# Score matrices of five pairs of key tiles per inner block of layer 2: seven quarter products in place of eight (Strassen), summed on VectorE

## The chip, the cores and the metric

The kernel runs on one core of a Trainium2 chip. The metric is the device time of one execution in microseconds (us), taken as the median of several runs. A profile of one further execution gives the time of every instruction on each engine: TensorE (PE for matmuls, PEld for its weight loads), VectorE (DVE), ScalarE (ACT), GpSimd (POOL), and the DMA queues, most of which are issued by SyncE (SP).

## The reference

Four graph layers are applied to 3327 nodes with 256 features. Each is an attention over the same adjacency matrix, followed by a residual sum and a layer norm. Cut to layer 2, which the change concerns:

```python
def _L2_gnn_ref(x, adj, Wq, bq, Wk, bk, Wv, bv):
    q = x @ Wq.T + bq
    k = x @ Wk.T + bk
    v = x @ Wv.T + bv
    scores = q @ k.T / sqrt(256)
    scores = where(adj > 0, scores, -9e15)
    attention = softmax(scores, axis=-1)
    return elu(attention @ v)

x = layernorm(x + _L0_gnn_ref(...))
x = layernorm(x + _L1_gnn_ref(...))
x = layernorm(x + _L2_gnn_ref(x, adj, ...))
x = layernorm(x + _L3_gnn_ref(...))     # three attention layers of its own
```

All of it is computed in float32. Layers 1 and 3 build their attention weights from sums of two vectors, without a score matrix; layers 0 and 2 need one.

## The kernel before

**Tiles.** The 3328 padded nodes are NT = 26 key tiles of 128 and NB = 7 query blocks of CH = 512 (the last one has 256). A layer is a loop over blocks `b`, and in a block over key tiles `j`; `steps` lists all (layer, block, tile) in order. "Pair p" below means key tiles 2p and 2p+1, of which a block has 13. "Inner blocks" are b = 1 to 5.

**One pair in layer 2.** `weights2` (L556) computes the transposed scores of one key tile with all queries of the block: two float32 matmuls (one for each half `h` of the 256 features, L563) of 128x128 keys from `FT` by 128x512 transformed queries `g`, summed in one PSUM bank `ps`. TensorE executes each float32 matmul as two instructions, so a pair takes 8 of them. ScalarE turns the bank into `ex` with an exponential (L571), and VectorE multiplies by the 0/1 mask into `e` (`masked`, L477). When both tiles of a pair are there, `sums` (L720, its four operations at L727 to L730) makes the four sums S1 to S4 of the quarters of `e`, 128x256 each, on VectorE. `products` (L751, its matmuls at L779) then multiplies the weights by the values `v`, as seven Strassen products, 14 matmuls of 128x128 or 128x129 (28 instructions), into the four banks `po` of the block. The sums of the values, `tsums`, are fetched from HBM by `fetch_tsum`.

**A block.** At a block's end `finish` runs as a generator, one `yield` further with each step of the next block. It joins the products (`joined`, L787, twelve or so VectorE operations that read PSUM and so free the `po` banks), then does ELU, residual and layer norm, and the scores of layer 3 (L591). `block2` (L515) prepares the transformed queries `g` of the next block from step 14 on (matmuls at L522, gT at L529, a maximum at L537, and a chain of small operations that ends in `off`).

**What sets the order.** The main loop calls `make_to(s + LA + 1)` with LA = 2, so that the weights of a tile are issued three steps ahead of the step that uses them. `make` (L1305) issues the weights and, at an odd tile, the sums. Only the first steps stand in an order written by hand; after that a scheduler orders each engine's instructions from the program's order, its own cost model and the free buffers. Each engine works through its instructions in that order. In layer 2 TensorE's order is: 8 score instructions of pair p+1, 28 product instructions of pair p-1 or p, and so on in turn.

**Buffers.** PSUM has two pools: `ps_o`, five banks, four of which a block's `po` occupy, and `ps_b`, three banks through which everything else rotates (`bank`, L66: `ps`, `pgq`, `psr`, `pn`). In SBUF the tag "a" (three buffers) holds the exponentials, "e" (five) the weights, "acc" (two) the sums `ssum`, "stage" (four) and "x4k" (two) larger intermediates. The pool `wts` holds weights of the layers, under tags of which "scratch0", "scratch1", "scratch2", "w_l1_w" and "w_l2_wvt" are 128x512 float32 each and not in use through the inner blocks of layer 2; "scratch1" and "w_l1_w" are loaded again for the last attention of layer 3 (`setup3`).

Of the kernel before, what the change touches and what calls it, by code (L numbers as in the profile page):

```python
# [8 lines left out]
F32 = mybir.dt.float32  # L9
# [4 lines left out]
AF = mybir.ActivationFunctionType  # L14
ALU = mybir.AluOpType
# [4 lines left out]
P = 128  # L20
D = 256
H = 128
LA = 2
CH = 512
# [9 lines left out]
def gnn_stack(ctx: ExitStack, tc: tile.TileContext, a: dict, N: int, out: bass.AP):  # L34
# [8 lines left out]
    nc = tc.nc  # L43
    NT = (N + P - 1) // P
    NP = NT * P
    NB = (NP + CH - 1) // CH
# [3 lines left out]
    def bw(b):  # L50
        return min(CH, NP - b * CH)
# [6 lines left out]
    wts = ctx.enter_context(tc.tile_pool(name="wts", bufs=1))  # L58
    cols = ctx.enter_context(tc.tile_pool(name="cols", bufs=2))
    mpool = ctx.enter_context(tc.tile_pool(name="mpool", bufs=2))  # L60
    work = ctx.enter_context(tc.tile_pool(name="work", bufs=2))
# [4 lines left out]
    def bank(name):  # L66
        return ps_b.tile([P, CH], F32, tag="pb", name=name)
# [3 lines left out]
    start = tc.manual_schedule(  # L71
        engines={engines.PE, engines.Activation, engines.DVE, engines.Pool}
    )
# [30 lines left out]
    FT = [big.tile([P, 2, CH], F32, name=f"ft{g}") for g in range(NB)]  # L104
# [28 lines left out]
    def rsqrt(dst, v, n, eng=nc.vector, tag="rs"):  # L133


        g = cols.tile([P, n], I32, tag=tag + "_g", name="rs_g")
        eng.tensor_scalar(g, v.bitcast(I32), -0.5, MAGIC, ALU.mult, ALU.add)
        y = g.bitcast(F32)
        vh = cols.tile([P, n], F32, tag=tag + "_v", name="rs_v")
        eng.tensor_scalar(vh, v, -0.5 * 0.375**3, None, ALU.mult)  # L140

        def step(out, q, c, f):

            if eng is nc.vector:
                eng.scalar_tensor_tensor(out, q, c, f, ALU.add, ALU.mult)
            else:
                h = cols.tile([P, n], F32, tag=tag + "_h", name="rs_h")
                eng.tensor_scalar(h, q, c, None, ALU.add)
                eng.tensor_tensor(out, h, f, ALU.mult)

        q = cols.tile([P, n], F32, tag=tag + "_q", name="rs_q")
        eng.tensor_tensor(q, y, y, ALU.mult)
        eng.tensor_tensor(q, q, v, ALU.mult)
        p = cols.tile([P, n], F32, tag=tag + "_p", name="rs_p")
        step(p, q, -10.0 / 3.0, q)
        z = cols.tile([P, n], F32, tag=tag + "_y", name="rs_y")
        step(z, p, 5.0, y)
        q = cols.tile([P, n], F32, tag=tag + "_q", name="rs_q")
        eng.tensor_tensor(q, z, z, ALU.mult)
        eng.tensor_tensor(q, q, vh, ALU.mult)  # L160
        step(dst, q, 1.5 * 0.375, z)
# [241 lines left out]
    def mask(b, j, n=1):  # L403
        wd = bw(b)
        return masks[b][:, j * wd : (j + n) * wd]
# [68 lines left out]
    def masked(b, j, t_):  # L474
        wd = bw(b)
        e = work.tile([P, CH], F32, tag="e", name="e", bufs=5)
        nc.vector.scalar_tensor_tensor(  # L477
            e[:, :wd], t_[:, :wd], 0.0, mask(b, j), ALU.add, ALU.mult
        )
        return e  # L480
# [32 lines left out]
    gq = {}  # L513

    def block2(b):  # L515

        wd = bw(b)
        g = work.tile([P, 2, CH], F32, tag="x4k", name="gT", bufs=2)
        for o in range(2):
            pm = bank("pgq")  # L520
            for h in range(2):
                nc.tensor.matmul(  # L522
                    pm[:, :wd],
                    w["G"][:, h, o * P : (o + 1) * P],
                    FT[b][:, h, :wd],
                    start=(h == 0),
                    stop=(h == 1),
                )
            nc.scalar.activation(  # L529
                g[:, o, :wd], pm[:, :wd], AF.Identity, bias=w["u"][:, o : o + 1]  # L530
            )
            yield

        gm = cols.tile([P, 2], F32, tag="gm", name="gm")
        nc.vector.tensor_reduce(  # L537
            gm, g[:, :, :wd], AX.X, ALU.max, apply_absolute_value=True
        )
        nc.vector.tensor_tensor(gm, gm, gm, ALU.mult)  # L540
        g1 = cols.tile([P, 1], F32, tag="g1", name="g1")
        nc.vector.tensor_tensor(g1, gm[:, 0:1], gm[:, 1:2], ALU.add)
        yield
        pn = bank("pn")
        nc.tensor.matmul(pn[:, :1], ones, g1, start=True, stop=True)
        yield
        n2 = cols.tile([P, 1], F32, tag="n2", name="n2")
        nc.vector.tensor_scalar(n2, pn[:, :1], TINY, None, ALU.max)
        off = cols.tile([P, 1], F32, tag="off", name="off")
        rsqrt(off, n2, 1)  # L550
        nc.vector.tensor_tensor(off, off, n2, ALU.mult)
        nc.vector.tensor_scalar(off, off, -1.0, 80.0, ALU.mult, ALU.add)
        nc.vector.tensor_scalar(off, off, 0.0, None, ALU.min)
        gq[b] = g, off

    def weights2(b, j):  # L556


        wd = bw(b)
        g, off = gq[b]  # L560
        ps = bank("ps")
        for h in range(2):
            nc.tensor.matmul(  # L563
                ps[:, :wd],
                FT[j // 4][:, h, (j % 4) * P : (j % 4 + 1) * P],
                g[:, h, :wd],
                start=(h == 0),
                stop=(h == 1),
            )
        t_ = work.tile([P, CH], F32, tag="a", name="ex", bufs=3)  # L570
        nc.scalar.activation(  # L571
            t_[:, :wd], ps[:, :wd], AF.Exp, bias=off, scale=1.0 / D**0.5
        )
        return masked(b, j, t_)
# [3 lines left out]
    class Gat:  # L578
# [75 lines left out]
        def weights(self, b, j):  # L654
            wd = bw(b)
            t_ = work.tile([P, CH], F32, tag="a", name="re", bufs=3)
            nc.scalar.activation(  # L657
                t_[:, :wd],
                self.u[b][:, :wd],
                AF.Relu,  # L660
                bias=self.nrh[:, j : j + 1],
                scale=self.th[:, j : j + 1],
            )
            if self.last and b == NB - 1:
                e = V[0][j]
            else:
                e = work.tile([P, CH], F32, tag="e", name="e", bufs=5)
            nc.vector.scalar_tensor_tensor(  # L668
                e[:, :wd],
                t_[:, :wd],  # L670
                self.rh[:, j : j + 1],
                mask(b, j),
                ALU.add,
                ALU.mult,
            )
            return e
# [6 lines left out]
    def strassen(L, b):  # L683
        return L.key == "2" or (L.key == "0" and 0 < b < NB - 1)
# [35 lines left out]
    def sums(b, e1, e2):  # L720

        hw = bw(b) // 2
        x = work.tile([P, 4, D], F32, tag="acc", name="ssum", bufs=2)
        s1, s2, s3, s4 = (x[:, i, :hw] for i in range(4))
        e11, e21 = e1[:, :hw], e1[:, hw : 2 * hw]
        e12, e22 = e2[:, :hw], e2[:, hw : 2 * hw]
        nc.vector.tensor_tensor(s3, e11, e21, ALU.subtract)  # L727
        nc.vector.tensor_tensor(s1, e21, e22, ALU.add)
        nc.vector.tensor_tensor(s2, s1, e11, ALU.subtract)
        nc.vector.tensor_tensor(s4, e12, s2, ALU.subtract)  # L730
        return e11, e12, e22, s1, s2, s3, s4
# [128 lines left out]
    def sum_weights(wt):  # L860
        b11, b12, b21, b22 = (wt[:, h, o * H : (o + 1) * H] for h in range(2) for o in range(2))
        t1, t2, t3, t4 = wsum
        nc.vector.tensor_tensor(t1, b12, b11, ALU.subtract)
        nc.vector.tensor_tensor(t3, b22, b12, ALU.subtract)
        nc.vector.tensor_tensor(t2, b22, t1, ALU.subtract)
        nc.vector.tensor_tensor(t4, t2, b21, ALU.subtract)
# [435 lines left out]
    steps = [(L, b, j) for L in layers for b in range(NB) for j in range(NT)]  # L1302
    made = deque()

    def make(s):  # L1305
        if s >= len(steps):
            return
        L, b, j = steps[s]
        if strassen(L, b) and j % 2 == 0 and kept.get((L.key, j // 2)) != b:
            fetch_tsum(L.key, b, j // 2)  # L1310
        if L.is_gat:
            made.append(L.gat.weights(b, j))
        else:
            made.append((weights0 if L.key == "0" else weights2)(b, j))
            if strassen(L, b) and j % 2:
                e2, e1 = made.pop(), made.pop()
                made.append(None)
                made.append(sums(b, e1, e2))
# [36 lines left out]
    for s, (L, b, j) in enumerate(steps):  # L1355
# [43 lines left out]
        if end:  # L1399

            k, h = divmod(2 * j, NT)
            for i in (h, h + 1):
                for o in range(2 if k else 1):
# [5 lines left out]
                        start=(i == 0),  # L1409
                        stop=(i == NT - 1),  # L1410
# [19 lines left out]
        elif not strassen(L, b):  # L1430
            for k in range(len(pos)):
# [4 lines left out]
                    start=(j == 0),  # L1436
                    stop=(j == NT - 1),
# [29 lines left out]
        begin = 2 if last and b == NB - 2 else 14  # L1467
        if L.is_gat and (b, j) == (0, 22):
            sum_weights(w[L.w])
        if j == (25 if L.key == "1" else 22) and not end:  # L1470
            while pending:
                advance()
# [85 lines left out]
```

## Time and profile before

| | |
|---|---|
| median of 3 runs | 2356.56 us (2355.24 to 2356.90) |
| the profiled execution, its own time | 2355.78 us |
| its span, first to last instruction | 2354.0 us |
| TensorE matmul, busy | 2335.3 us, 99% of the span, 12257 instructions |
| TensorE weight load, busy | 1917.4 us, 81% |
| VectorE, busy | 1665.8 us, 71%, 4500 instructions |
| ScalarE, busy | 1221.5 us, 52%, 1976 instructions |
| GpSimd, busy | 40.0 us, 2% |
| mean granted TensorE clock | 0.998 |
| layer 2, first to last score matmul (L563) | 804.2 to 1385.3 us |

Busy time is time in which an engine has at least one instruction in flight; matmuls overlap, so that the sum of their durations is larger than the busy time. The distance between the starts of two runs of like instructions tells more about TensorE's rate than the duration of one. The granted clock is the share of its full rate that TensorE was allowed.

### The profile page before, as it was taken

The page shows a single profiled execution, that of the slowest core. Times are in us where ns is not written, and L with a number is a line of the kernel's source. Part 1 is how long each engine was busy: PE and PEld are TensorE (multiplying, and loading weights), DVE is VectorE, ACT ScalarE, POOL GpSimd, SP SyncE. Part 2 cuts the span into 40 slices and gives each one's busy share as a digit, 9 for nine tenths or more (in the row PEclk, how much of TensorE's full clock was granted, in tenths as well). Part 3 has the DMA queues.
Part 4 walks back from the last instruction along what each step waited for, and adds up shares of the span by engine and source line. Part 5 has one row for each costly group of instructions (what it writes and reads, how often), then busy time and mean ns, then how long its engine had stood idle before and what let it go on. Part 6 is the DMA issues. An engine that isn't in the chain of part 4 may idle for free.

```text
span 2354.0 us, 33990 instructions
## 1 busy us (share of the span) xinstructions
PE 2335.3 (99%) x12257; PEld 1917.4 (81%) x12257; DVE 1665.8 (71%) x4500; ACT 1221.5 (52%) x1976; POOL 40.0 (2%) x156
## 2 busy tenths in 40 slices
PE   9999999999999999999999999999999999999997
PEld 6788888888888777767677798888888888888887
DVE  7789999867777666567567586666756666666676
ACT  4667777755555422222222255565665555655554
POOL 0000000000000000000000000000000000000000
PEclk9999999999999999999999999999999999999999
DMA  8655555423222312212212221210211111132111
GB/s 275 196 187 184 167 199 191 151 75 83 74 81 60 108 54 88 79 54 86 76 46 74 83 88 48 73 56 26 71 53 43 43 51 52 50 101 70 61 44 46
DMA packets 147293, 214.72 MB, mean 91 GB/s; under 512 B 76093, under 2 KB 101172, under 8 KB 142516
## 3 DMA queue, kind: packets, MB, share of 16 engines
q1 hardware_dynamic: 146852, 212.28, 28.1%
q8 instruction: 96, 1.57, 0.3%
q14 instruction: 73, 0.60, 0.1%
q10 hardware_dynamic: 272, 0.26, 0.0%
HBM read 167.53 MB, written 28.19 MB: 83 GB/s over the span
## 4 chain that ended last, share of the span: by engine, by line
PE 94%; DVE 3%; ACT 1%; DMA 1%; issue 1%; POOL 0%; SPq 0%; POOLq 0%; DVEq 0%; ACTq 0%
PE po L1432 48%; PE po L779 19%; PE ps L563 12%; PE ps L492 6%; PE pproj L890 3%; PE po L1405 1%; PE pv L1148 1%; PE pgq L522 1%; ACT re L657 1%; DMA stage<-in_adj_a 1%; PE pk L353 0%; DMA turned<-planes 0%; PE pq L317 0%; DVE e L668 0%; PE pproj L1062 0%
## 5 line engine op out<-in xcount | busy, mean ns | idle before, releaser
L1432 PE MATMUL po<-v,e 128*128 128x257 f32 x5616 | 1248.6, 381 | 1.5 <-ACT p L1026 1.3
L1432 PEld LDWEIGHTS po<-v,e 128*128 128x128 f32 x5616 | 1057.7, 190 | 165.3 <-issue 9.3
L657 ACT ACTIVATE re<-u,nrh,th 128x512 f32<-128x512 f32 (+1 forms) x728 | 556.1, 780 | 483.9 <-DVE e L668 478.0
L668 DVE SCALAR_TENSOR_TENSOR e<-re,rh,mask 128x512 f32<-128x512 f32 (+1 forms) x702 | 501.2, 718 | 347.6 <-PE po L1432 311.6
L563 PE MATMUL ps<-gT,ft 128*128 128x512 f32 (+1 forms) x728 | 307.4, 563 | 0.0
L571 ACT ACTIVATE ex<-ps,off 128x512 f32<-128x512 f32 (+1 forms) x182 | 119.1, 655 | 356.6 <-PE ps L563 356.0
L779 PE MATMUL po<-tsums,ssum 128*128 128x128 f32 (+1 forms) x1794 | 249.3, 275 | 0.0
L477 DVE SCALAR_TENSOR_TENSOR e<-ex,mask 128x512 f32<-128x512 f32 (+1 forms) x182 | 118.6, 651 | 164.1 <-ACT ex L571 163.3
L563 PEld LDWEIGHTS ps<-gT,ft 128*128 128x128 f32 x728 | 132.0, 190 | 114.5 <-issue 111.7
L779 PEld LDWEIGHTS po<-tsums,ssum 128*128 128x128 f32 x1794 | 224.5, 192 | 0.7 <-ACT y L982 0.3
L779 PEld LDWEIGHTS po<-v,e 128*128 128x128 f32 x1196 | 169.3, 191 | 67.4 <-issue 54.7
L779 PE MATMUL po<-v,e 128*128 128x129 f32 x1196 | 182.4, 275 | 0.0
L505 ACT ACTIVATE ex<-ps,rq 128x512 f32<-128x512 f32 (+1 forms) x183 | 118.7, 651 | 116.8 <-PE ps L492 107.5
L492 PE MATMUL ps<-ft,ft 128*128 128x512 f32 (+1 forms) x312 | 142.5, 561 | 0.0
L506 DVE SCALAR_TENSOR_TENSOR e<-ex,mask 128x512 f32<-128x512 f32 (+1 forms) x183 | 116.8, 644 | 34.2 <-ACT ex L505 33.2
L449 DVE CUSTOM_DVE_ANT_0 acc<-acc,stage 128x1024 uint16<-128x1024 uint16 (+1 forms) x168 | 108.7, 647 | 12.3 <-DMA stage<-in_adj_a 9.2
L779 PE MATMUL po<-tsums,e 128*128 128x128 f32 x598 | 92.3, 275 | 0.4 <-DVE y L821 0.4
L779 PE MATMUL po<-v,ssum 128*128 128x128 f32 x598 | 92.3, 275 | 0.0
L436 ACT ACTIVATE mask<-pos 128x1024 uint8<-128x1024 bf16 (+1 forms) x87 | 86.4, 993 | 2.1
L435 ACT ACTIVATE pos<-stage 128x1024 bf16<-128x1024 int32 (+1 forms) x87 | 85.6, 984 | 1.2 <-DVE e L506 1.2
L779 PEld LDWEIGHTS po<-tsums,e 128*128 128x128 f32 x598 | 79.3, 192 | 0.6 <-issue 0.6
L779 PEld LDWEIGHTS po<-v,ssum 128*128 128x128 f32 x598 | 79.4, 192 | 0.1
(295 smaller groups left out, 1899.7 us busy)
## 6 DMA issues: line engine op xcount, KB each, us to landing
mask<-mask_d SPq DMA_DIRECT2D x30, 1664.0 KB
stage<-in_adj_a SPq DMA_DIRECT2D x78, 512.0 KB
tsums<-t_d SPq DMA_DIRECT2D x152, 256.5 KB
mask_d<-mask SPq DMA_DIRECT2D x6, 1664.0 KB
u<-s_d SPq DMA_DIRECT2D x24, 256.0 KB
xT<-in_xT SPq DMA_DIRECT2D x10, 512.0 KB
mask<-mask_d SPq DMA_DIRECT2D x5, 832.0 KB
t_d<-tsums SPq DMA_DIRECT2D x14, 256.5 KB
```

Source lines behind the costliest of these rows:

```text
L436: nc.scalar.activation(mask(b, j, 2), t_[:, : 2 * wd], AF.Sign)
L449: nc.vector.tensor_tensor(acc, acc, st[:, h * wd : (h + 1) * wd], ALU.add)
L477: nc.vector.scalar_tensor_tensor(e[:, :wd], t_[:, :wd], 0.0, mask(b, j), ALU.add, ALU.mult)
L492: nc.tensor.matmul(ps[:, :wd], FT[j // 4][:, 0, (j % 4) * P : (j % 4 + 1) * P], FT[b][:, 1, :wd], start=True, stop=True,)
L505: nc.scalar.activation(t_[:, c], ps[:, c], AF.Exp, scale=rq[:, j : j + 1])
L506: nc.vector.scalar_tensor_tensor(e[:, c], t_[:, c], 0.0, mask(b, j)[:, c], ALU.add, ALU.mult)
L563: nc.tensor.matmul(ps[:, :wd], FT[j // 4][:, h, (j % 4) * P : (j % 4 + 1) * P], g[:, h, :wd], start=(h == 0), stop=(h == 1),)
L571: nc.scalar.activation(t_[:, :wd], ps[:, :wd], AF.Exp, bias=off, scale=1.0 / D**0.5)
L657: nc.scalar.activation(t_[:, :wd], self.u[b][:, :wd], AF.Relu, bias=self.nrh[:, j : j + 1], scale=self.th[:, j : j + 1],)
L668: nc.vector.scalar_tensor_tensor(e[:, :wd], t_[:, :wd], self.rh[:, j : j + 1], mask(b, j), ALU.add, ALU.mult,)
L779: nc.tensor.matmul(o, x, y, start=(p == 0 and g not in banks[:i]), stop=(p == NT // 2 - 1 and g not in banks[i + 1 :]),)
L1432: nc.tensor.matmul(pos[k], es[:, k * P : (k + 1) * P], V[L.i % 2][j], start=(j == 0), stop=(j == NT - 1),)
```

## The change

For pairs 2, 4, 6, 8 and 10 of each inner block, the scores of a pair are computed as one 256x512 matrix with Strassen's scheme in Winograd's form: the 256 keys by 256 features and the 256 features by 512 queries are each cut into four quarters, seven products of quarters (128x128 by 128x256) are made, and eleven of their sums give the four quarters of the scores. Details that the working needs:

- `block2` also makes four sums T1 to T4 of the quarters of `g` (128x256 each) for an inner block, into a buffer of the tag "stage".
- `sum_keys` makes four sums S1 to S4 of the quarters of a pair's keys (128x128 each), once for each of the five pairs, into the five `wts` buffers named above, where they stay for all inner blocks.
- `pair_weights` issues the seven products (14 TensorE instructions of 128x256, in three banks: m1 with m2, m6 with m7, m5 with m4, and m3 in half a bank), copies m1 out of PSUM on ScalarE, and does the seven sums with the other products on VectorE. The results are in two buffers of tag "a", in which the exponential then works in place. The mask follows as before.
- `make` issues the first four products of a pair at the odd tile before it, the other three at the pair's own tiles. TensorE's order in the built program becomes: 8 score instructions of an ordinary pair, m1, m2, m6, m7 of the next pair, the 28 instructions of `products`, m5, m4, m3, the 28 of the next `products`, and again.

```diff
@@ block2
         gq[b] = g, off
+        if 0 < b < NB - 1:
+            yield
+            x = work.tile([P, 4, D], F32, tag="stage", name="gsums", bufs=4)
+            t1, t2, t3, t4 = (x[:, i, :] for i in range(4))
+            b11, b12, b21, b22 = (g[:, h, i * D : (i + 1) * D] for h in range(2) for i in range(2))
+            nc.vector.tensor_tensor(t1, b12, b11, ALU.subtract)
+            nc.vector.tensor_tensor(t3, b22, b12, ALU.subtract)
+            nc.vector.tensor_tensor(t2, b22, t1, ALU.subtract)
+            nc.vector.tensor_tensor(t4, t2, b21, ALU.subtract)
+            gsum[b] = t1, t2, t3, t4
+    gsum, ksum = {}, {}
+    KPAIRS = {2: "scratch0", 4: "scratch1", 6: "scratch2", 8: "w_l1_w", 10: "w_l2_wvt"}
+    def by_pairs(L, b, p):
+        return L.key == "2" and 0 < b < NB - 1 and p in KPAIRS
...
+    def sum_keys(p):
+        a11, a12, a21, a22 = keys_of(p)
+        x = wts.tile([P, 4, P], F32, tag=KPAIRS[p], name="ksum")
+        s1, s2, s3, s4 = (x[:, i, :] for i in range(4))
+        nc.vector.tensor_tensor(s3, a11, a21, ALU.subtract)
+        nc.vector.tensor_tensor(s1, a21, a22, ALU.add)
+        nc.vector.tensor_tensor(s2, s1, a11, ALU.subtract)
+        nc.vector.tensor_tensor(s4, a12, s2, ALU.subtract)
+        ksum[p] = s1, s2, s3, s4
+    def pair_weights(b, p):
...
+        x = [work.tile([P, CH], F32, tag="a", name="ex2", bufs=3) for _ in range(2)]
+        c11, c12, c21, c22 = (t[:, i * D : (i + 1) * D] for t in x for i in range(2))
+        def two(*pairs):
+            ps = bank("ps2")
+            for i, (l, r) in enumerate(pairs):
+                nc.tensor.matmul(ps[:, i * D : (i + 1) * D], l, r, start=True, stop=True)
+            return ps[:, :D], ps[:, D:]
+        def weights(k):
+            nc.scalar.activation(x[k], x[k], AF.Exp, bias=off, scale=1.0 / D**0.5)
+            return masked(b, 2 * p + k, x[k])
+        m1, m2 = two((a11, b11), (a12, b21))
+        m6, m7 = two((s2, t2), (s3, t3))
+        nc.scalar.copy(c22, m1)
+        nc.vector.tensor_tensor(c11, c22, m2, add)
+        nc.vector.tensor_tensor(c22, c22, m6, add)
+        nc.vector.tensor_tensor(c21, c22, m7, add)
+        yield
+        m5, m4 = two((s1, t1), (a22, t4))
+        nc.vector.tensor_tensor(c12, c22, m5, add)
+        nc.vector.tensor_tensor(c22, c21, m5, add)
+        nc.vector.tensor_tensor(c21, c21, m4, sub)
+        yield weights(1)
+        m3, _ = two((s4, b22))
+        nc.vector.tensor_tensor(c12, c12, m3, add)
+        yield weights(0)
@@ make
+        if j % 2 and by_pairs(L, b, (j + 1) // 2):
+            pairs[b, j + 1] = pair_weights(b, (j + 1) // 2)
+            next(pairs[b, j + 1])
...
+        elif by_pairs(L, b, j // 2):
+            made.append(next(pairs[b, j - j % 2]))
+            if j % 2:
+                e1, e2 = made.pop(), made.pop()
+                made.append(None)
+                made.append(sums(b, e1, e2))
@@ main loop
+        if L.key == "2" and (b * NT + j + 6 - NT) / 2 in KPAIRS:
+            sum_keys((b * NT + j + 6 - NT) // 2)
```

## The prediction

> **What bounds the kernel now.** I read the page's shares first, then the chain that ended last, then the windows of layer 2 and the timelines of TensorE and VectorE in one block's turn.
>
> ```profile
> PE 2335.3 (99%) x12257; PEld 1917.4 (81%) x12257; DVE 1665.8 (71%) x4500; ACT 1221.5 (52%) x1976; POOL 40.0 (2%) x156
> ...
> PE 94%; DVE 3%; ACT 1%; DMA 1%; issue 1%; POOL 0%; SPq 0%; POOLq 0%; DVEq 0%; ACTq 0%
> ```
>
> TensorE is never without work, and the chain that ends last is TensorE's own order for 94% of the span. The next view is the windows by stage; columns after the length are busy us of PE, PEld, DVE, ACT, POOL, then clock, DMA share and GB/s.
>
> ```profile
> 1080.00:1165.00 85.00, 85.00 (x462) 59.66 (x461) 55.73 (x160) 21.89 (x37) 0.00 (x0) 1.00 0.19 61
> ```
>
> In an inner stretch of layer 2, PE is busy for all 85 us at full clock and DVE for 55.7 (66%). The list of waits has no wait of a TensorE instruction on DVE or ACT over 1.2 us in total in layer 2. So there a TensorE instruction less is time less, as long as VectorE stays ahead. What an instruction costs is read from distances of starts (columns: start, us, then the group):
>
> ```profile
> 905.66 3.60 PE L563 MATMUL ps<-gT,ft 128*128 128x512 f32 x8
> 909.10 0.83 PE L779 MATMUL po<-v,e 128*128 128x129 f32 x6
> ...
> 912.22 3.60 PE L563 MATMUL ps<-gT,ft 128*128 128x512 f32 x8
> ...
> 1350.77 1.89 PE L563 MATMUL ps<-gT,ft 128*128 128x256 f32 x8
> 1352.50 0.61 PE L779 MATMUL po<-v,e 128*128 128x129 f32 x4
> ```
>
> Eight instructions of 128x512 take 909.10 - 905.66 = 3.44 us (430 ns each), the 28 of `products` 912.22 - 909.10 = 3.12 us, so a pair takes 6.56 us. The last block of the layer has scores of 128x256, the shape that the change uses: eight take 1352.50 - 1350.77 = 1.73 us, 216.3 ns each, though each loads its own weights.
>
> VectorE's queue, where it is fullest, and where it is calm:
>
> ```profile
> 906.42 0.42 DVE L819 TENSOR_TENSOR p<-p,po 128x256 f32<-128x256 f32 x1
> 906.76 0.41 DVE L820 TENSOR_TENSOR p<-p,po 128x256 f32<-128x256 f32 x1
> 907.21 0.42 DVE L821 TENSOR_TENSOR p<-p,po 128x256 f32<-128x256 f32 x1
> ...
> 930.43 0.42 DVE L728 TENSOR_TENSOR ssum<-e 128x256 f32<-128x256 f32 x1
> 930.89 0.42 DVE L729 TENSOR_TENSOR ssum<-ssum,e 128x256 f32<-128x256 f32 x1
> ...
> 934.54 0.69 DVE L477 SCALAR_TENSOR_TENSOR e<-ex,mask 128x512 f32<-128x512 f32 x1 [2.77 <-ACT ex L571]
> ```
>
> A sum of 128x256 takes 0.42 us, read from PSUM or not. The next starts 0.34 us later if it needs nothing of it, 0.46 if it does. After a block's end DVE has no gap from 904.8 to 928.5 us in its timeline; from then on it waits 2.8 us in each pair for the next exponential.
>
> **What the skill says.** "VectorE: DVE Perf Modes", section on the perf-mode tier table: a float32 sum of two tensors has only the plain mode, SBUF or PSUM alike; its errata section prices it at (N+151)/0.96 ns, 424 ns for 256. The trace agrees (423). The same page's section on the DRAIN says the next operation starts when the pipe is empty; here it starts after 0.34 of 0.42 us when independent, and I use the measured distance. "Perfetto Trace Analysis", section on the most-contended engine: matmul busy time misleads because matmuls overlap; the trace agrees (the 128x256 row's mean is longer than its 216 ns distance), hence the distances. "PSUM — Partial Sum Buffer", section on bank collisions: engines are to be kept apart by bank, so whoever reads m1 waits for m2 too. I assume that; no row of before tells it.
>
> **The change part by part.**
>
> *Scores removed and added.* Per changed pair 8 instructions of 128x512 go (3.44 us) and 14 of 128x256 come (14 x 0.2163 = 3.03). The difference is 0.41 us; 5 blocks x 5 pairs = 25 times gives 10.3 us. Weight loads rise from 8 to 14 per pair; they are covered by the 216 ns distance just read, which has one load per instruction.
>
> *VectorE's additions.* 7 sums with PSUM in each of 25 pairs, 4 sums of 128x256 in each of 5 blocks, 4 of 128x128 for each of 5 pairs: 175 x 0.42 + 20 x 0.42 + 20 x 0.28 (the row of L817) = 87.5 us of busy time. An inner block lasts 13 x 6.56 + 3.44 (L522) + about 0.2 = 88.9 us; at 66% DVE is busy for 58 of it, plus 17.5 makes 76 of the new 86.9 (87%). There is room on the average. On the path it costs nothing unless a result comes late, which needs a layout.
>
> *Calm cycle, laid out from the built program's order.* Time 0 is the start of an ordinary pair's scores. PE: scores to 3.44, m1 m2 to 4.31, m6 m7 to 5.17, products to 8.29, m5 m4 to 9.16, m3 to 9.59, products to 12.71. In the trace ACT starts 0.2 us after PE, DVE 0.03 after ACT. DVE masks the second tile till 5.1; six sums interleaved (three with PSUM, three of `ssum`) till 7.3; m5, m4, m3 are taken from 9.4 to 11.1. Two exponentials in place (714 ns is the row of L649, which also reads SBUF) end at 12.1, two masks at 13.6, four sums at 15.4. The products that need them start in the next cycle, at 12.71 + 5.17 = 17.9. Lead: 2.5 us. Banks: the last m5/m4 read is at 11.1, its bank is wanted at 14.4.
>
> *Full cycle, the first of a block.* I kept the old trace to 908.40 (the joining ends there and frees `po`) and set the new DVE queue behind it: 0.34 us for an independent sum, 0.60 for a mask, 0.2 for small links of a chain. Pair 2's three PSUM sums fall between 911.5 and 913.2, the four others between 915.2 and 917.1, its masks end at 919.4, its `ssum` at 922.2; PE wants them at 923.6. Pair 3's are there at 926.0, wanted at 928.0; pair 4's at 935.8, wanted at 936.3, its last sum (S4) only in the final products, some 2.6 us after. Pair 5 has 1.9 us again. The backlog is carried two cycles and paid in the third, without a wait of PE. This 0.5 us is the tightest place.
>
> *Cycle with block2.* DVE's maximum (L537, 1.22 us) waits for gT as before, with T1 to T4 behind it; the masks behind those are due at 10.8 and wanted for products at 17.5. Another wait, of n2 on `pn`, holds DVE from 15.1 to 16.4 in that count; the sums of pair 10 end at 23.5, wanted at 24.1.
>
> *ScalarE.* 25 copies of 128x256 (0.37 us, row of L805); it is at 26% in the window. Exponentials are equal in number. Free, and if VectorE's queue were late they would be late with it.
>
> *Buffers and queues.* "a", "e", "acc" come free in the layouts before they are wanted by 2 us or more. On SP the loads of the two weights in "scratch1" and "w_l1_w" now stand in block 5 instead of earlier, behind the last reader of the key sums; behind them in SP's queue are fetches of `tsums`, which wait for later products anyway. Zero; if not, a late `tsums` costs one pair at most, some 2 us. POOL's order is unchanged.
>
> *Sum.* -10.3 us on the profiled execution: span 2354.0 to 2343.7, its own time 2355.78 to 2345.5. Its time is 0.8 us below the median of the runs, so the median goes to 2346.3. Bounds of the main case: the distance of 216.3 ns is read to 1 or 2 ns, 25 x 14 x 2 ns = 0.7 us; runs spread by 0.9.
>
> **The rivals.**
>
> *A, stalls at block starts.* The tightest lead is 0.5 us; if the 14 new PSUM sums of pairs 2 and 4 step at 0.46 instead of 0.34, DVE is 1.7 us later, and PE waits about 1 us per block: 5 us back, 2351.3. For it: DVE without a gap for 24 us before any addition. Against it: the queue interleaves new sums with old ones, so few follow what they need.
>
> *B, slower: VectorE's queue sets the pace.* m3 ends a chain of sum, exponential, mask and four sums, some 6 us in the calm layout. If DVE takes those sums late (head of its queue waiting for an exponential while banks wait behind it, three banks in all), PE stops in each changed pair. From 0.41 us per pair it eats the gain; at 1 us it gives 25 x (1.0 - 0.41) = +15, 2371. Against it: the leads of 2.5 us in calm cycles.
>
> *C, no gain.* If the 14 products stepped at 245 ns (3.44 / 14), for instance because weight loads between different operands were not covered, the time would stay 2356.6. Against it: 216 ns in the last block, and products at 111 ns with other weights each time.
>
> **How the numbers follow.** Main case 0.68, A 0.16, B 0.11, C 0.05. A change of 0.2% (4.7 us) is about what a measurement of this kernel can tell from none. Faster by over 0.2% takes the main case and a half of A: 0.76. Within 0.2%: the rest of A and C: 0.13. Slower: B, 0.11. The range runs from the main case less its bounds, 2344.8, to A with 1 us more, 2352.5: 0.84.
>
> **What would show it.** Right: the 14 products start 216 ns apart, changed pairs take 6.15 us, no PE wait on DVE in layer 2, DVE near 87% there. A: gaps before `products` of pairs 3 to 5 of each block only. B: gaps in every changed pair, ended by DVE L617 to L626 or the sums. C: the distance itself. The forecast is wrong if DVE's distances with PSUM operands are longer than in the joining, or if the rotation of three banks makes m6 m7 or an ordinary score wait.

## The result, and the profile after

| | before | after |
|---|---|---|
| median of 7 runs each | 2356.51 us | 2349.31 us (2346.35 to 2349.77) |
| ratio | 1 | 0.9968, 95% interval [0.9958, 0.9977] |
| profiled execution, its own time | 2355.78 us | 2346.35 us |
| its span | 2354.0 us | 2344.6 us |

The changed kernel is 7.2 us faster, 0.31%, where 10.3 us were forecast. Its profiled execution is 9.4 us shorter, but it was the fastest of its seven runs. So two things are to be explained: where the 9.4 us come from, and why the median has less. In the kernel after, L606 holds the seven products, L616 to L626 their sums, L610 the exponential in place, L615 the copy, L636 the ordinary scores, L852 `products`, L910 and L917 the turning of a finished tile (L837 and L844 before), and L1135 the projection that reads it (L1062).

The page's first lines, and its chain:

```profile
span 2344.6 us, 34571 instructions
...
PE 2325.3 (99%) x12407; PEld 1946.4 (83%) x12407; DVE 1722.1 (73%) x4715; ACT 1233.3 (53%) x2001; POOL 41.3 (2%) x156
...
PE 94%; DVE 3%; ACT 1%; DMA 1%; issue 1%; POOL 0%; POOLq 0%; SPq 0%; DVEq 0%; ACTq 0%
```

TensorE has 150 matmul instructions more and 10.0 us less busy time, and the chain is its own order as before. VectorE has 56 us more. The timeline of TensorE through one cycle of an ordinary and a changed pair (start, us, group):

```profile
905.06 3.60 PE L636 MATMUL ps<-gT,ft 128*128 128x512 f32 x8
908.49 1.03 PE L606 MATMUL ps<-gT,ft 128*128 128x256 f32 x4
909.36 1.03 PE L606 MATMUL ps<-gsums,ksum 128*128 128x256 f32 x4
910.22 0.83 PE L852 MATMUL po<-v,e 128*128 128x129 f32 x6
...
913.35 0.60 PE L606 MATMUL ps<-gsums,ksum 128*128 128x256 f32 x2
913.78 0.59 PE L606 MATMUL ps<-gsums,ft 128*128 128x256 f32 x2
914.21 0.59 PE L606 MATMUL ps<-gT,ksum 128*128 128x256 f32 x2
914.64 0.83 PE L852 MATMUL po<-v,e 128*128 128x129 f32 x6
...
917.77 3.60 PE L636 MATMUL ps<-gT,ft 128*128 128x512 f32 x8
```

From 908.49 to 910.22 are 1.73 us, from 913.35 to 914.64 are 1.29: 3.02 us for the 14 instructions, 216 ns each. The cycle takes 917.77 - 905.06 = 12.71 us, as laid out.

The windows of the first inner block, of this kernel and then of the one before:

```profile
906.00:993.00 87.00, 87.00 (x511) 67.95 (x510) 67.73 (x202) 24.33 (x43) 0.00 (x0) 1.00 0.24 77
```
```profile
906.00:995.00 89.00, 89.00 (x480) 62.24 (x479) 56.90 (x163) 22.58 (x38) 0.00 (x0) 1.00 0.24 76
```

TensorE (first number after the length) is busy for the whole of both. A block takes 86.99 us from its L522 to that of the next, in place of 89.05. VectorE (third) rises from 56.9 to 67.7 us, which is 78% and not the 87% of the forecast.

To see where time is won, I compare the starts of TensorE instructions that no change touches. Between two of them in layer 2 (the norm L545 of block 0, at 878 us, and the transpose L708 in the last block, at 1366 us after and 1377 before) the kernel after gains 10.29 us. Outside this layer it should then run in parallel with the kernel before, and it does, to 0.05 us, from 1377 to 1983 us. Then, at one place in the second of layer 3's three attentions, it loses 0.9 us, and from there to the end 0.5. Ahead of layer 2 it had 0.6 us of lead, from layer 0, where the change does nothing; so the 9.4 us of this execution are 0.6 + 10.3 - 0.9 - 0.5 within rounding, and 0.6 of them are chance.

The list of TensorE's waits names that place. Its lines that matter, after and then before, with the totals over the whole kernel:

```profile
PE pasum L464 <- DVE af L460: 1.2, 1, 1.2
PE pproj L1135 <- DVE pT L917: 1.2, 1, 1.2
```
```profile
PE pproj L1062 <- DVE pT L844: 0.3, 1, 0.3
```

None of the waits in either list, those left out here too, lies in layer 2. The wait on the turned tile, 1.2 us in place of 0.3, is at the place just named, in layer 3, which the change doesn't touch. There `finish` sends a finished block through a transposing DMA ("turns" it), VectorE copies it, and the projection multiplies it. This turn, of the last full block of the second attention, is called the last turn below. What happened to the DMA shows in its busy share over 11 us around the issue (40 slices of 0.275 us, in tenths; the issue, the start of SP's instruction, is at 1988.80 after, at 1999.65 before), with the queues of the window:

```profile
DMA  0000000000000000009990004999970000000000
...
q1 hardware_dynamic: 2080, 0.52, 33.6%
q8 instruction: 1, 0.02, 0.7%
```
```profile
DMA  0000000000000000029999996000000000000000
...
q1 hardware_dynamic: 2080, 0.52, 21.0%
q14 instruction: 1, 0.01, 0.2%
```

In the kernel before the 2080 packets run in one piece. In the kernel after a transfer of the kind "instruction" falls among them 1.17 us after the issue, and they stand still for some three slices. They end 4.39 us after the issue in place of 3.18, about the 1.2 us of the wait. (The kernel before meets a smaller one, of 8 KB on q14, 3.17 us after the issue, at the very end of its packets; its copy then starts 3.96 us after the issue where turns that meet nothing have 3.75, and this goes with its own wait of 0.3.) The page has 97 transfers on q8 with 1.59 MB, 16 KB each. In layer 3 they come 26.6 us apart on average (21 to 31), and between two of them TensorE starts 128 matmul instructions on average, so 256 with the weight loads; 24,814 of the whole kernel by 97 is 256 too. So I take them for TensorE's instruction stream (inferred, no view names the engine). By this reading, the 150 matmuls and their loads that the change adds shift where this stream is fetched, through the rest of the kernel.

### The profile page after: what moved, and what is told of

Read it like the earlier page. It is cut to its first block, busy times and chain, and to the rows that moved or that the text cites. A ratio compares the mean times of both kernels' runs of the same rounds, so it can differ in the third digit from the quotient of the medians.

```text
span 2344.6 us, 34571 instructions
## 1 busy us (share of the span) xinstructions
PE 2325.3 (99%) x12407; PEld 1946.4 (83%) x12407; DVE 1722.1 (73%) x4715; ACT 1233.3 (53%) x2001; POOL 41.3 (2%) x156
## 3 DMA queue, kind: packets, MB, share of 16 engines
q8 instruction: 97, 1.59, 0.3%
## 4 chain that ended last, share of the span: by engine, by line
PE 94%; DVE 3%; ACT 1%; DMA 1%; issue 1%; POOL 0%; POOLq 0%; SPq 0%; DVEq 0%; ACTq 0%
PE po L1519 48%; PE po L852 20%; PE ps L636 9%; PE ps L492 6%; PE ps L606 3%; PE pproj L963 3%; PE po L1492 1%; PE pv L1221 1%; PE pgq L522 1%; ACT re L730 1%; DMA turned<-planes 1%; PE pk L353 0%; PE pq L317 0%; DVE e L741 0%; PE pproj L1135 0%
## 5 line engine op out<-in xcount | busy, mean ns | idle before, releaser
L852 PE MATMUL po<-tsums,ssum 128*128 128x128 f32 (+1 forms) x1794 | 249.3, 275 | 0.0
L852 PEld LDWEIGHTS po<-tsums,ssum 128*128 128x128 f32 x1794 | 224.5, 192 | 0.7 <-ACT y L1055 0.3
L636 PE MATMUL ps<-gT,ft 128*128 128x512 f32 (+1 forms) x528 | 216.2, 551 | 0.0
L852 PEld LDWEIGHTS po<-v,e 128*128 128x128 f32 x1196 | 169.3, 191 | 45.9 <-issue 33.0
L644 ACT ACTIVATE ex<-ps,off 128x512 f32<-128x512 f32 (+1 forms) x132 | 85.1, 646 | 224.3 <-PE ps L636 223.7
L852 PE MATMUL po<-v,e 128*128 128x129 f32 x1196 | 182.3, 275 | 0.0
L636 PEld LDWEIGHTS ps<-gT,ft 128*128 128x128 f32 x528 | 96.0, 190 | 79.0 <-issue 72.7
L852 PE MATMUL po<-v,ssum 128*128 128x128 f32 x598 | 92.3, 275 | 0.0
L852 PE MATMUL po<-tsums,e 128*128 128x128 f32 x598 | 92.1, 275 | 0.0
L610 ACT ACTIVATE ex<-ex,off 128x512 f32<-128x512 f32 x50 | 33.9, 718 | 107.7 <-DVE ex L626 99.8
L852 PEld LDWEIGHTS po<-v,ssum 128*128 128x128 f32 x598 | 79.4, 192 | 0.1
```

Source lines behind the costliest of these rows:

```text
L636: nc.tensor.matmul(ps[:, :wd], FT[j // 4][:, h, (j % 4) * P : (j % 4 + 1) * P], g[:, h, :wd], start=(h == 0), stop=(h == 1),)
L852: nc.tensor.matmul(o, x, y, start=(p == 0 and g not in banks[:i]), stop=(p == NT // 2 - 1 and g not in banks[i + 1 :]),)
```

## The experiments

All times are given beside those of the kernel before in the same comparison: 2355.7 us (first four), 2355.6 (next four), 2355.3 (last three). "Layer 2" is the gain between the two instructions named above.

**The same kernel again.**

> The changed kernel once more, nothing edited. The first profile of it showed layer 2 shorter by 10.3 us and no wait of TensorE there, but the median gain was 7.2 us. Theory (all of the gain is TensorE time in layer 2, and what is missing lies in waits on transfers in other layers that differ from execution to execution): the layer is again 10.2 to 10.4 us shorter, and the median lies 7 to 10 us below the kernel before. Rival (VectorE's added sums make TensorE wait in some executions): the profile shows waits of TensorE in layer 2 where the time is high.

Measured: 2348.42 us, ratio 0.9966 [0.9953, 0.9978]. Layer 2 gains 10.29 us again. The wait on the turned tile is there again with 1.7 us; the transfer came 1.33 us after the issue. Before layer 2 this execution is 2.3 us behind that of the kernel after, from layer 0, where the profiles of all kernels but the two with a longer start differ by up to 2.6 us.

**Without the sums.** The seven sums and the copy are left out; the exponentials read the banks of m1/m2 and m5/m4, so that the weights aren't those of the scores.

```diff
-        m1, m2 = two((a11, b11), (a12, b21))
+        m12 = two((a11, b11), (a12, b21))
...
-        nc.vector.tensor_tensor(c11, c22, m2, add)
-        nc.vector.tensor_tensor(c22, c22, m6, add)
-        nc.vector.tensor_tensor(c21, c22, m7, add)
...
-        yield weights(1)
+        yield weights(1, m54)
```

> Leaves out the seven sums on VectorE and the copy on ScalarE of each changed pair; the exponentials read two of the product banks as they are, so the weights of these pairs are not the scores'. All 14 TensorE instructions stay. Theory (the sums are wholly covered): layer 2 as long as in the changed kernel within 0.5 us, total within 2 us of it. Rival (the sums cost the missing 3 us): 3 us or more below the changed kernel.

Measured: 2347.49 us, ratio 0.9963 [0.995, 0.9975]; layer 2 gains 10.12. VectorE's busy time in the block goes back to 56.9 us and layer 2 wins nothing: the sums are covered. Of the 3 us that the median lacks, 1.9 stay with none of the seven sums. This kernel too has the wait on the turned tile, 1.6 us; here the 16 KB transfer begins 3.18 us after the issue, when the packets are all but through, and the last few, of 4 bytes, come behind it and end at 4.16 us.

**Each sum twice.** A second sum of the same size into an unused tile, behind each of the seven:

```diff
+        def again(m, op):
+            junk = work.tile([P, D], F32, tag="ejunk", name="junk", bufs=2)
+            nc.vector.tensor_tensor(junk, g[:, 0, :D], m, op)
...
         nc.vector.tensor_tensor(c11, c22, m2, add)
+        again(m2, add)
```

> After each of the seven sums a second one of the same size, PSUM operand and bank, into a scratch tile: 35 more VectorE operations per inner block, 35 x 0.34 = 11.9 us. By the trace the tightest lead, pair 4 in each block, is 1.1 us plus up to 2.6 us until the last sum is used, and 14 doubled sums by then come to 4.8 us. Theory (cover exists and is used up between one and two times the sums): TensorE begins to wait at pairs 4 to 6 of each block, 1 to 4 us per block, total 5 to 20 us above the changed kernel. Rival (ample cover): no wait, same time. Rival (VectorE already sets the pace): 12 us per block, 60 in all.

Measured: 2350.94 us, ratio 0.9979 [0.997, 0.9988]; layer 2 gains 5.06, so the doubling costs 5.2 us. The window of the block and TensorE's waits:

```profile
906.00:993.00 87.00, 86.22 (x502) 66.83 (x501) 76.12 (x233) 24.35 (x43) 0.00 (x0) 1.00 0.24 74
```
```profile
PE ps L647 <- ACT ex L655: 3.9, 5, 0.8
```
```profile
946.04 0.69 ACT L655 ACTIVATE ex<-ps,off 128x512 f32<-128x512 f32 x1 [9.76 <-DVE ex L632]
```

VectorE has reached 76.1 of 87 us, the 87% that the forecast had put to the change itself, and there TensorE does stop: once in each inner block, 0.8 us, at an ordinary score (L647) whose bank ScalarE hasn't read yet, while ScalarE, by the profile, waits for a late sum (L632). These five stops are 3.9 of the 5.2 us; the other 1.3 are in no wait of the list. In the first block the stop is at the scores of pair 7, later than the pairs 4 to 6 that were expected. So rival A's price, 1 us a block, is what twice the sums cost. The median follows layer 2's gain to 0.3 us, and so lies only 1.6 us above the changed kernel's, under the 5 that were expected at least.

**Eight plain quarter products.** The same shapes and order without Strassen: two products added up in PSUM for each quarter of the scores. The sums of keys and queries are still made.

```diff
+                    nc.tensor.matmul(
+                        ps[:, i * D : (i + 1) * D],
+                        keys[k][h],
+                        g[:, h, i * D : (i + 1) * D],
+                        start=(h == 0),
+                        stop=(h == 1),
+                    )
```

> The five pairs with eight plain quarter products of the same shape 128x256, accumulated in PSUM, without the VectorE sums of the products; the sums of keys and queries are still made. 16 TensorE instructions of 128x256 in place of 8 of 128x512. Theory (the gain is the one product of eight saved, 0.43 us per pair): layer 2 within 1 us of the kernel before, total within 0.1% of it. Rival (the narrower shape or the other order of instructions brings part of the gain): faster than the kernel before by 3 us or more.

Measured: 2356.39 us, ratio 1.0001 [0.9993, 1.0009]; layer 2 loses 0.50 us. Rival C falls: 200 more instructions at half the size cost 0.50 us / 200 = 2.5 ns each, weight loads included. The gain is the product that is saved.

**Shifting the instruction stream, by small matmuls at the start.** Twelve 128x1 matmuls in the warm-up of the kernel after, and sixteen in that of the kernel before, were meant to move the transfers at next to no cost:

```diff
+    for _ in range(12):
+        nc.tensor.matmul(turned[:, :1], ones, ones[:, :1], start=True, stop=True)
```

> The changed kernel with 12 more float32 matmuls of 128x1 among the warm-up matmuls at the start (48 TensorE instructions with their weight loads). Layer 2 is 10.3 us shorter in each profile of the change, but TensorE waits 1.2 and 1.7 us for a turned tile in the last block of the second attention of layer 3, where the kernel before waited 0.3. In those profiles a 16 KB transfer on the queue of kind instruction begins 1.2 to 1.3 us after that turning transfer is issued, in the middle of its packets; the transfers of that queue come every 28 us, as often as TensorE passes 256 instructions, so they look like TensorE's own instructions. Theory (this collision): 48 instructions earlier in the stream move it 5 us forward, the wait falls to 0.3 us or below, and the total is 1 to 1.5 us below the changed kernel, less what the 12 matmuls cost at the start (0 to 1.5). Rival (the wait has another cause, such as the two weight loads that the change moves on the SP queue): the wait stays at 1.2 to 1.7 us.

> The kernel before with 16 more float32 matmuls of 128x1 at the start (64 TensorE instructions): there the 16 KB transfer lies 8.7 us after the turning transfer is issued, and 64 instructions at 0.108 us move it to about +1.7 us, into its packets. Theory: the wait of TensorE for the turned tile rises from 0.3 to 1.0 to 1.8 us in a kernel that has nothing of the change; total 0.5 to 3 us above the kernel before. Rival (the moved weight loads): the wait stays at 0.3.

Measured: 2350.92 us, ratio 0.9978 [0.9968, 0.9988], and 2366.83 us, ratio 1.0042 [1.0029, 1.0055]. The cost was not small. TensorE's timeline at the start of the first of the two:

```profile
4.62 5.12 PE L82 MATMUL turned<-ones 128*128 128x1 f32 x24
9.60 2.05 PE L96 MATMUL turned<-part,count 128*128 128x128 f32 x8
```

The next work starts 4.98 us later, 0.2 us an instruction (each loads weights, which takes 0.33 us here and 0.19 later), and by layer 2 the kernel is 6.3 us behind the kernel after. Within the profiles both did what they were to do: in the first the transfer comes before the turning transfer and the wait is gone; in the second one comes 3.3 us after the issue, ahead of the last packets, at the last turn and at layer 1's, and the kernel before loses 1.39 us and 1.66. But the medians can't be read for it.

**Other numbers of pairs.** Six pairs add pair 12, whose key sums share a buffer with pair 2's and are made anew in each block. Three and four pairs leave the others as ordinary scores.

```diff
-    KPAIRS = {2: "scratch0", 4: "scratch1", 6: "scratch2", 8: "w_l1_w", 10: "w_l2_wvt"}
+    KPAIRS = {2: "scratch0", 4: "scratch1", 6: "scratch2", 8: "w_l1_w", 10: "w_l2_wvt", 12: "scratch0"}
...
+        if L.key == "2" and b < NB - 2 and j == 24:
+            sum_keys(2)
+        if L.key == "2" and 0 < b < NB - 1 and j == 16:
+            sum_keys(12)
```
```diff
-    KPAIRS = {2: "scratch0", 4: "scratch1", 6: "scratch2", 8: "w_l1_w", 10: "w_l2_wvt"}
+    KPAIRS = {6: "scratch2", 8: "w_l1_w", 10: "w_l2_wvt"}
```
```diff
-    KPAIRS = {2: "scratch0", 4: "scratch1", 6: "scratch2", 8: "w_l1_w", 10: "w_l2_wvt"}
+    KPAIRS = {2: "scratch0", 6: "scratch2", 8: "w_l1_w", 10: "w_l2_wvt"}
```

> Pair 12 of each inner block is changed too; its key sums share a buffer with those of pair 2, so both are made anew in each block (8 more sums of 128x128 per block on VectorE). Theory (0.41 us of TensorE per changed pair as long as VectorE stays ahead): layer 2 another 2.0 us shorter, 12.3 us below the kernel before, and the 16 KB transfer moves away from the turning one (60 more instructions), so the total is 2343 to 2345 us. Rival (VectorE's queue at the end of a block, where the joining comes, is full): TensorE waits at the block's end and the gain is less than 1 us or gone.

> Pairs 6, 8 and 10 alone are changed, in the calmer part of each block. Theory: 15 x 0.41 = 6.2 us off layer 2, 2349.5 us. Rival (stalls at the block's start eat part of what pairs 2 and 4 bring): as fast as the changed kernel or faster, and more than 0.41 us per pair.

> The changed kernel with four pairs (2, 6, 8, 10) in place of five. Layer 2 gains 20 x 0.412 = 8.2 us in place of 10.3, and the instruction transfer comes some 4 us later, out of the turning transfer. Theory 'the missing gain follows the wait': median 8.2 us under the kernel before, 2347.4, which is under that of five pairs though it does less of the change. Theory 'the loss of about 3 us comes with the change itself, whatever the wait': 2350 to 2350.5.

Measured: six pairs 2343.68 us, ratio 0.995 [0.9937, 0.9963], layer 2 gains 11.85 (30 x 0.412 would be 12.36; the 0.5 between was not followed up). Three pairs 2349.51 us, 0.9975 [0.9965, 0.9984], layer 2 gains 6.18. Four pairs 2347.76 us, 0.9968 [0.9957, 0.998], layer 2 gains 8.23, and the median 7.5. None has the wait on the turned tile. Four pairs are as fast as five, and three give up 4.1 us of layer 2 but only 1.1 of the median. So five pairs lose something that the others do not. Six pairs are the best version of this study, 11.9 us under the kernel before.

**Shifting the stream without a cost.** Since halves of a score cost nothing (the eight products showed it), a few ordinary scores of layer 2 are cut in two. That is 16 matmuls more in the kernel after, and 20 in the kernel before:

```diff
+        cut = D if b == 3 and j in (2, 3, 6, 7, 10, 11, 14, 15) else wd
+        for lo in range(0, wd, cut):
+            for h in range(2):
+                nc.tensor.matmul(
+                    ps[:, lo : lo + cut],
...
+                    g[:, h, lo : lo + cut],
```

> The changed kernel, with the scores of eight ordinary tiles of block 3 of layer 2 cut into two halves of 128x256 each: the same work, 32 TensorE instructions of 256 in place of 16 of 512, so 16 matmuls more in the program and next to no time (200 such instructions cost 0.5 us in the run with eight quarter products). What it moves is the place at which TensorE's instruction transfers fall: about 4 to 5 us earlier at the last turn of layer 3, so out of the turning transfer, without the long start of the run with twelve small matmuls. Theory 'the missing gain follows that wait': no wait on the turned tile, and the layer's 10.2 us arrive at the end, median about 10.2 us under the kernel before, 2345 to 2346. Theory 'the wait is only what the profiles show of it, the rest is lost elsewhere': 0.9 to 1.4 us better than the changed kernel, 2347 to 2347.5. Theory 'the wait costs nothing': the changed kernel's time, 2348.5 to 2349.

> The kernel before, with the scores of ten tiles of layer 2 (eight of block 2, two of block 3) cut into halves in the same way: 20 matmuls more and about 0.1 us of work. By the earlier shifts (about 0.32 us a matmul) the instruction transfer that came 8.7 us after the issue of the last turning transfer comes about 2.3 us after it, so inside it. Theory 'the missing gain follows the wait': a wait of about 1 us on the turned tile in its profile, median 1 to 3 us above the kernel before, 2356.7 to 2358.7. Theory 'the wait costs nothing': 2355.7. If no wait is in its profile, the shift was mis-sized and the run tells nothing.

Measured: the kernel after, with the scores cut, 2345.21 us, ratio 0.9957 [0.9944, 0.9969]: 10.1 us under the kernel before, with 10.21 gained in layer 2. Four of its five runs lie below the lowest of the twelve runs of the kernel after and its repetition (2346.34); the intervals of the two ratios overlap. The kernel before, with the scores cut, 2357.34 us, ratio 1.0007 [0.9998, 1.0015]: 2.1 us slower, though its interval just reaches 1. The DMA's share around the last turning transfer and TensorE's wait behind it, first of the kernel after with cut scores (window 1985 to 1996):

```profile
DMA  0020000000000000089999990000000000000000
```
```profile
1993.62 1.13 PE L1137 MATMUL pproj<-w_l_w,pT 128*128 128x256 f32 x4
```

Then of the kernel before with cut scores (window 1998 to 2009):

```profile
DMA  0000002000991999992000000000000000000000
...
q8 instruction: 1, 0.02, 0.5%
q14 instruction: 1, 0.01, 0.2%
```
```profile
2005.76 1.13 PE L1064 MATMUL pproj<-w_l_w,pT 128*128 128x256 f32 x4 [1.12 <-DVE pT L846]
```

In the first the instruction transfer (the lone 2 in the third slice) comes before the turning transfer, whose packets run in one piece, and the projection starts without a wait. In the second it (the lone 2 in the seventh slice) comes 0.38 us after the issue, just ahead of the first packets (2.3 us were aimed at, in their midst). SP's turning instruction takes 1.99 us in place of 1.57, the packets have a gap of a slice and end 3.77 us after the issue in place of 3.18, and the projection waits 1.12 us in place of 0.27. Some of that delay is another's: the 8 KB transfer on q14, which the kernel before had too, now begins at 3.45 us, and the last packets come behind it. The wait of the changed kernel can be taken away, and given to the kernel before, with not a sum of Strassen's moved. Nor is it made by the two weight loads that the change puts later in SP's queue: the first kernel has them there and no wait, the second hasn't and waits.

Over the thirteen profiles, 19 turns of 2080 packets meet a 16 KB transfer that begins 0.3 to 2.9 us after their issue (turns with other packets beside theirs left out). Their packets end 3.45 to 4.97 us after the issue; those of the 246 turns that meet no instruction transfer end at 3.17 to 3.35. TensorE waits at only three of the 19, the last turns of the kernel after, of its repetition and of the kernel before with cut scores. In the kernel after with cut scores a turn at 1746 us ends at 4.97 and nothing waits. The collisions are common; the last turn is where one costs time.

All kernels but the two with a longer start, in us against the kernel before (at the last turn: against its wait of 0.27 there, so that -0.3 is none):

| kernel | layer 2 | last turn | median | median less layer 2 |
|---|---|---|---|---|
| after | -10.29 | +0.90 | -7.2 | 3.1 |
| after, again | -10.29 | +1.46 | -7.3 | 3.0 |
| no sums | -10.12 | +1.28 | -8.2 | 1.9 |
| before, cut scores | +0.10 | +0.86 | +2.1 | 2.0 |
| sums twice | -5.06 | -0.23 | -4.8 | 0.3 |
| eight products | +0.50 | -0.31 | +0.7 | 0.2 |
| six pairs | -11.85 | -0.29 | -11.9 | -0.1 |
| three pairs | -6.18 | -0.28 | -6.1 | 0.1 |
| four pairs | -8.23 | -0.27 | -7.5 | 0.7 |
| after, cut scores | -10.21 | -0.27 | -10.1 | 0.1 |

The four kernels with the wait lack 1.9 to 3.1 us of their layer 2; the six without lack 0.7 at most. A part of what is lacking lies outside the span of instructions: an execution's time is 1.74 to 1.86 us more than its span wherever the record has both for the kernel before, but up to 2.79 for the kernel after, and 2.12 to 2.82 in seven of the thirteen executions of the kernel before with cut scores. What it is spent on no profile shows.

## Why the prediction was right, and where it was wrong

The median lies in the forecast range by the room that was left for rival A, whose stalls didn't come: the main case was 2346.3 us, and the 2349.31 measured lie 3.0 above it, outside its bounds of 0.7 and 0.9. So the gain of layer 2 was right to 0.1 us, and that the range held is luck.

*Scores removed and added: right.* 14 instructions took 3.02 us where 3.03 were forecast. The 25 pairs gained 10.29 us where 10.3 were. The distance of 216.3 ns, read from the last block of the kernel before, carried over to other operands and other weight loads. Three and four pairs scale with it (15 x 0.412 = 6.18, 20 x 0.412 = 8.24).

*VectorE's additions: right that they are covered, wrong in size.* Leaving them out won nothing. But the forecast added 17.5 us to a block by multiplying durations of 0.42 us, and the block shows 10.8 us more. The working itself had read that independent sums start 0.34 us apart, and had used this in the layouts; the average was made with the wrong one. With 0.34 it would have been some 13 us a block, still more than measured. The prediction also set its 0.34 us against the DRAIN section of "VectorE: DVE Perf Modes" in the Trainium skill; that section adds that an operation which isn't held starts earlier, so page and trace don't contradict each other here. In the trace the sums interleave as the layout said:

```profile
911.21 0.42 DVE L801 TENSOR_TENSOR ssum<-e 128x256 f32<-128x256 f32 x1
911.55 0.42 DVE L617 TENSOR_TENSOR ex<-ex,ps 128x256 f32<-128x256 f32 x1
911.88 0.42 DVE L802 TENSOR_TENSOR ssum<-ssum,e 128x256 f32<-128x256 f32 x1
912.21 0.42 DVE L618 TENSOR_TENSOR ex<-ex,ps 128x256 f32<-128x256 f32 x1
```

Sums that read PSUM (L617, L618) step at 0.33 us like those of SBUF, and so they do where each follows another directly, in the run with doubled sums (944.26, 944.60, 944.92, 945.26). This is the number on which rival A hung (0.46 in its case).

*The tightest lead: right in place, on the safe side in size.* Pair 4's last sum and the products that want it:

```profile
934.11 0.43 DVE L803 TENSOR_TENSOR ssum<-e,ssum 128x256 f32<-128x256 f32 x1
```
```profile
935.64 0.83 PE L852 MATMUL po<-v,e 128*128 128x129 f32 x6
```

The lead is 935.64 - 934.54 = 1.1 us where 0.5 was forecast. VectorE's first gap after the block's start is at 938.85, when the backlog is paid, as the layout had it:

```profile
939.83 0.42 DVE L621 TENSOR_TENSOR ex<-ex,ps 128x256 f32<-128x256 f32 x1 [0.98 <-PE ps L606]
```

*The cycle with block2, the copies on ScalarE, the buffers: no wait of TensorE in layer 2 is in the list, so their zeros hold.* What was assumed of the banks is seen too: in the second cycle m1 ends at 921.80 and m2 at 922.23, and ScalarE's copy of m1 starts at 922.27.

*The rivals.* A and B don't happen with the change; both lie near. With the sums doubled, one stop in each block appeared, and layer 2 lost 5.2 us, A's price, with B's mechanism (a bank waiting behind ScalarE, which waits behind the sums), though not in each pair. C is excluded by the 216 ns and by the eight products.

*The sum: the step that failed.* It set everything outside layer 2 to zero: "Zero; if not, a late `tsums` costs one pair at most", with transfers named for which TensorE didn't come to wait. The working counted 6 instructions more per pair for their own time alone. It didn't ask what else a changed count moves. The count set where TensorE's instruction transfers fall, and one fell into the turning transfer. The term was 0; it measured 2 to 3 us in the medians, of which the profiles show 0.9 to 1.5 at the last turn. Shown by experiment is that moving the transfer out and in removes and makes the wait, and that the median goes with it in all ten kernels of the table. Not settled is why the medians lose one or two us more than the profiles show at that place. Part of it is the time outside the span: the profiled execution of the kernel before with cut scores has 0.7 us more span and 1.4 us more of its own time. The two profiles of the changed kernel differ by 2.3 us in layer 0 alone, and other transfers may collide in executions that no profile shows.

## What to carry to other kernels

In a stage that one engine fills, a price read as the distance of starts in a row of the same shape holds to a percent, and a second engine's load should be summed from distances too, not from durations. When a gain of a few us is right in its stage and missing at the end, compare the starts of untouched instructions along the whole kernel, and look at the place where they part. In these runs a changed number of TensorE instructions moved the instruction transfers far behind the change, and it cost time where a DMA was waited for with little to spare. Starting such a DMA earlier than its calm time asks for should help; that was not tried here.

## What the runs showed of the hardware

- An instruction transfer of 16 KB, about one in 256 TensorE instructions, holds up a transposing DMA of 2080 packets: its end moved from 3.18 us after the issue to 4.39 (after), 4.97 (after, again) and, with the transfer ahead of the last packets only, 4.16 (no sums). The transposing instruction itself takes 1.57 us in SP's queue undisturbed, and 2.68 in the kernel after.
- float32 matmuls of 128x1 at the kernel's start, each with a weight load of 0.33 us, take 0.2 us per instruction, about as long as one of 128x256 in the middle of it (0.216, with a load of 0.19).
- Cutting float32 matmuls of 128x512 into two of 128x256, with a weight load for each, costs 2.5 ns for each instruction added (0.50 us by 200 with eight products; 0.10 by 40 in the kernel before with cut scores).
- Sums of 128x256 on VectorE were added to a queue that is 64% busy for 0.28 us of busy time each (10.8 us by 39 instructions), against 0.42 us of duration.
